# A four-layer attention network: queries, keys and values of two layers as seven products of halves

## The chip, the cores and the metric

The kernel runs on one core of one Trainium2 chip. The metric is the device time of one execution in microseconds (us); the time given is the median of several runs. The core has five instruction streams that work side by side and wait for each other by semaphores: PE (TensorE, the matrix products), DVE (VectorE), ACT (ScalarE), POOL (GpSimd) and SP (SyncE, here only for starting transfers).

## What is computed

The input x is 2 images of 512 channels and 32 x 32 = 1024 positions. Four layers follow one another; layers 0 and 1 are not touched by the change (layer 0: deformable attention with a learned bias and an MLP; layer 1: linear attention). Layers 2 and 3 are two attention blocks of one form:

```python
def layer(x, gn_w, gn_b, qkv_w, qkv_b, proj_w, proj_b):   # layer 2: 8 groups; layer 3: 32 groups
    xn = group_norm(x) * gn_w + gn_b                      # x: (2, 512, 1024)
    q, k, v = qkv_w @ xn + qkv_b                          # each (2, 512, 1024), 8 heads of 64
    attn = softmax(q.T @ k * 64 ** -0.5)                  # per head, 1024 x 1024
    out = v @ attn.T                                      # (2, 512, 1024)
    return x + proj_w @ out + proj_b
```

Everything is float32.

## The kernel before

An image is held in SBUF as 4 tiles of 128 channels x 1024 positions (`self.xs[b][t]`). P is 128, C 512, CT 4, N 1024, HF 512, DH 64, NB 8; b counts images, t or c tiles of channels, h halves of 512 positions.

Layers 2 and 3 each run `attention` (from line 945). It calls `queries_keys_values` (982), then branches on a flag, computed on the chip, that says whether the logits are small enough to leave out the maximum of the softmax: with these data it always takes `heads_bounded` (1123), and `heads_general` is not executed.

`queries_keys_values` for each image: the norm (`group_norm`, 1110) writes 4 tiles; each block of 128 x 512 takes one subtraction and scaling on DVE (line 1117) and then the addition of the bias on ACT (1120). For each t the queries and then the keys are made: per half of the positions one PSUM accumulation over the 4 channel tiles (line 1016, 4 products of 128x128 weights with 128x512 data), taken out by DVE with bias and the factor 1/8 for a query (1024), or by ACT with the bias for a key (1028). POOL squares each finished 128x1024 tile (1032) and DVE takes block maxima of it (1034); from these the flag is made at the fourth block of the values (1046 to 1061). The values follow, 8 blocks of 128 positions x 512 channels, again 4 products each (1064), taken out by DVE with the bias `vb` (1071). The statistics of image 1 (`channel_means`, `group_means`, lines 1087 to 1105) are computed in the middle of image 0's first products; two small matmuls with `avg` (1094, 1101) average over a group.

`heads_bounded` works in 16 units: image b, pair of heads p, half h. A unit has 8 steps n. In each, PE makes the scores of 128 keys against 512 queries for both heads (line 1146), ACT takes the exponential out of PSUM (1150), POOL and DVE add the exponentials up (1155 to 1164), and PE, two steps later, multiplies them with the values (1175). PSUM holds 2 score tiles. At the end ACT and DVE add the two halves of o into the memory of the queries (1184, 1185). In step 4 of the next unit `divide` follows: PE sums over keys (1192), ACT copies one half (1196), DVE adds the other, takes the reciprocal and multiplies (1197, 1198, 1200). After all 16 units come the 8 projections (598), each added to x by DVE (607); in layer 2 the statistics of layer 3 are computed beside them, in layer 3 each piece of x is sent to DRAM at once.

The order on an engine is the order of the program where `manual_schedule` names the engine (DVE in `queries_keys_values`, PE in `heads_bounded`); elsewhere a scheduler of the framework places instructions when the kernel is built. An engine runs its instructions in that order and waits at the first that is not ready.

Layer 0's MLP already has the scheme that the change extends: `left_sums` (623), `right_sums` (631) and `seven` (638), with this table of left and right operand:

```python
SEVEN = {"P1": (0, 0), "P2": (1, 2), "P3": (6, 3), "P4": (3, 6), "P5": (2, 4), "P6": (4, 5), "P7": (5, 1)}
```

The left matrix has quarters a11, a12, a21, a22 and three sums S2, S3, S4 (index 0 to 6; S1 takes the place of a21), the right one quarters r0 to r3 and three sums. Each product covers half of the contraction, 2 instead of 4 channel tiles.

The weights of layer 2 and 3 (`attention_weights`, 930) are loaded by SP: 4 tiles of 128 x 1536 for queries, keys and values and 4 of 128 x 512 for the projection; layer 2's while the MLP of layer 0 runs, layer 3's while layer 2 runs.

Of the kernel before, what the change touches and what calls it, by code (L numbers as in the profile page):

```python
# [36 lines left out]
    ("gn_w2", CT), ("gn_b2", CT), ("qb2", CT), ("kb2", CT), ("pb2", CT),  # L37
    ("gn_w3", CT), ("gn_b3", CT), ("qb3", CT), ("kb3", CT), ("pb3", CT),
# [14 lines left out]
class Net:  # L53
# [569 lines left out]
    def left_sums(self, eng, w):  # L623

        a11, a12, a21, a22, s2, s3, s4 = (w[:, i] for i in range(7))
        eng.tensor_tensor(s3, a11, a21, ALU.subtract)
        eng.tensor_tensor(a21, a21, a22, ALU.add)
        eng.tensor_tensor(s2, a21, a11, ALU.subtract)
        eng.tensor_tensor(s4, a12, s2, ALU.subtract)
# [22 lines left out]
    def mlp0(self):  # L652
# [5 lines left out]
        with ExitStack() as ctx:  # L658
# [7 lines left out]
            def weights(n):  # L666
                got = []
                for name in ("mlp_w1", "mlp_w2"):
                    w = wpool.tile([P, 7, 2, 2 * P], F32, tag=name, name=f"{name}_{n}")
                    nc.sync.dma_start(w[:, 0:4], io[name][n % CT])  # L670
                    self.left_sums(nc.gpsimd, w)
# [258 lines left out]
    def attention_weights(self, pool, k: int, name: str):  # L930

        got = []
        for t in range(CT):
            src = self.io[f"l{k}_{name}"][t]
            got.append(pool.tile(list(src.shape), F32, tag=name, name=f"{name}{k}{t}"))
            self.nc.sync.dma_start(got[-1], src)
        return got
# [7 lines left out]
    def attention(self, k: int, qkv, proj, out, meanwhile=lambda: None):  # L945
# [3 lines left out]
        with ExitStack() as ctx:  # L949
            one = self.pool(ctx, f"a{k}")  # L950
            vb = one.tile([P, C], F32, tag="vb", name=f"vb{k}")
            nc.sync.dma_start(vb, self.io[f"l{k}_vb"].partition_broadcast(P))
# [3 lines left out]
            for b in range(B):  # L956
                qs = [one.tile([P, N], F32, tag=f"q{b}{t}", name=f"q{k}{b}{t}") for t in range(CT)]
                ks = [one.tile([P, N], F32, tag=f"k{b}{t}", name=f"k{k}{b}{t}") for t in range(CT)]
                v = one.tile([P, NB, C], F32, tag=f"v{b}", name=f"v{k}{b}")
                data.append((qs, ks, v))  # L960
            small_logits, got = self.queries_keys_values(k, qkv, vb, ones, data, meanwhile)
# [3 lines left out]
            with self.tc.If(small_logits > 0) as cmp:  # L965
                self.heads_bounded(k, ones, data, proj, out)
            with cmp.Else():
                self.heads_general(k, data)
                with ExitStack() as ctx2:
                    ps = self.pool(ctx2, f"a{k}_ps_p", 2, psum=True)  # L970
# [11 lines left out]
    def queries_keys_values(self, k, qkv, vb, ones, data, meanwhile):  # L982
# [4 lines left out]
        nc = self.nc  # L987
        with ExitStack() as ctx:
            act = self.pool(ctx, f"a{k}_x", 2)
            small = self.pool(ctx, f"a{k}_s", 2)  # L990
            squares = self.pool(ctx, f"a{k}_sq")
            ps = self.pool(ctx, f"a{k}_ps", 6, psum=True)
            ps_g = self.pool(ctx, f"a{k}_psg", 1, psum=True)
            flag = small.tile([1, B], F32, tag="flag", name=f"flag{k}")
            with self.tc.manual_schedule(engines={mybir.EngineType.DVE}):
                xns = [self.group_norm(k, 0, act)]
                for b in range(B):
                    xn = xns[b]
                    qs, ks, v = data[b]
                    late = []  # L1000
                    cm = squares.tile([P, 2, CT, DH], F32, tag="cm", name=f"cm{k}{b}")
                    for t in range(CT):
                        if b == 0 and t == 1:
                            for c in range(CT):
                                self.channel_means(k, 1, c)
                            self.means_tiles(k, 1)
                            for _ in self.group_means(k, 1, ps_g.tile([P, 2, CT], F32, tag="g0", name=f"gm{k}")):
                                pass
                            xns.append(self.group_norm(k, 1, act))
                        for i, y in enumerate((qs[t], ks[t])):  # L1010
                            at = i * C + t * P
                            for h in range(2):
                                cut = slice(h * HF, (h + 1) * HF)
                                acc = ps.tile([P, HF], F32, tag="ps", name=f"qk{i}p{k}{b}{t}{h}")
# [423 lines left out]
```

## Time and profile before

| what | value |
|---|---|
| median of 3 runs | 3492.95 us (3492.63 to 3493.12) |
| the profiled execution | 3491.61 us |
| its span in the profile | 3489.8 us |
| granted TensorE clock, mean | 0.996 |
| layer 0's attention | 0 to about 2089 us |
| layer 0's MLP | to 2474 us |
| layer 1 | 2474 to 2547 us |
| layer 2: queries, keys, values | 2548.7 to 2720.6 us |
| layer 2: attention and projection | 2721.5 to 3017.7 us |
| layer 3: queries, keys, values | 3019.2 to 3191.4 us |
| layer 3: attention, projection, output | 3192.2 to 3489.8 us |

The profile is one execution on the chip, told from its start in microseconds. A row of a group of instructions has the line of the program, the engine, the operation, what it writes and reads, the shapes and the count, then busy us and the mean in ns, then the idle time of the engine ahead of it and what ended that idle time. A row of waits has the engine and the tile that waited, what it waited for, the total, the number of times and the longest. A row of the chain or of the order in time has start and length in us. A float32 product of the program shows as two matmul records and two weight loads (LDWEIGHTS, "PEld"), which overlap with matmuls. A record's busy time includes its way through the array, so a dense sequence is priced by the distance of starts and not by the mean of one.

### The profile page before, as it was taken

Reading aid. Unit: us, or ns where it says so; the run is one execution under the profiler, and the core shown is the slowest. Engines: PE = TensorE matmul, PEld = TensorE weight load, DVE = VectorE, ACT = ScalarE, POOL = GpSimd, SP = SyncE. Lnnn points to the kernel's source line nnn. Section 1 sums busy time; section 2 is a strip of 40 time slices with the busy share of each in tenths; the row PEclk is TensorE's granted clock in tenths of the full one; section 3 lists DMA queues with packets and bytes.
Section 4 is the critical chain, followed back from the end, with each engine's and each line's share of the span. In section 5 each row is a group of like instructions: output and inputs, shape, how many; then the busy total and the mean of one; then the engine's idle time right before and its main releaser. Section 6 shows DMA issues by size and latency. Waiting matters only on the chain.

```text
span 3489.8 us, 59510 instructions
## 1 busy us (share of the span) xinstructions
PE 3433.0 (98%) x25152; PEld 1234.1 (35%) x25152; DVE 2235.6 (64%) x2393; ACT 2012.0 (58%) x2093; POOL 2016.5 (58%) x1512
## 2 busy tenths in 40 slices
PE   7999999999999999999999999999999999999999
PEld 2333333333333333333333334444644333443333
DVE  6877767767767578768766755565542566423774
ACT  5877877887887587887887741111120565102661
POOL 4777777787786577787788873332121344012441
PEclk9999999999999999999999999999999999999999
DMA  6877777787786677787888751110000000000001
GB/s 153 157 144 155 153 153 145 155 162 146 152 162 131 121 154 146 153 163 144 177 161 160 152 147 65 48 38 23 1 3 0 37 1 1 16 0 1 1 1 50
DMA packets 104108, 343.14 MB, mean 98 GB/s; under 512 B 12816, under 2 KB 14480, under 8 KB 101520
## 3 DMA queue, kind: packets, MB, share of 16 engines
q0 software_dynamic: 73296, 266.90, 40.4%
q1 hardware_dynamic: 29520, 70.21, 6.7%
q8 instruction: 202, 3.31, 0.4%
q10 hardware_dynamic: 1008, 2.06, 0.2%
q14 instruction: 82, 0.67, 0.1%
HBM read 67.79 MB, written 4.46 MB: 21 GB/s over the span
## 4 chain that ended last, share of the span: by engine, by line
PE 90%; DVE 7%; ACT 1%; issue 1%; POOL 0%; DMA 0%; DVEq 0%; ACTq 0%; POOLq 0%
PE hp L486 45%; PE o L1175 6%; PE s L1146 6%; DVE h L455 3%; PE qk0p L1016 3%; PE pb L598 3%; PE vp L1064 3%; PE qk1p L1016 3%; PE sim L518 3%; PE m_0P L647 1%; PE m_7P L647 1%; PE m_6P L647 1%; PE m_4P L647 1%; PE m_3P L647 1%; PE m_1P L647 1%; PE m_5P L647 1%
## 5 line engine op out<-in xcount | busy, mean ns | idle before, releaser
L486 PE MATMUL hp<-h,w 128*32 128x512 f32 x16384 | 1830.9, 593 | 5.6 <-DVE h L455 3.6
L455 DVE CUSTOM_DVE_ANT_1 h<-tx,bank 128x1024 f32<-128x1024 f32 x1024 | 1181.0, 1216 | 332.1 <-PE hp L486 309.0
L491 ACT ACTIVATE h<-hp,magb 128x1024 f32<-128x1024 f32 x1024 | 1122.0, 1111 | 416.5 <-PE hp L486 415.4
L486 PEld LDWEIGHTS hp<-h,w 128*32 128x32 f32 x16384 | 542.4, 110 | 1216.8 <-issue 1121.8
L478 POOL DMA_DIRECT2D h<-h x509 | 452.7, 1027 | 390.6 <-ACT h L497 333.2
L504 POOL TENSOR_TENSOR h<-h,h 128x1024 f32<-128x1024 f32 x255 | 613.9, 2408 | 21.3
L502 POOL TENSOR_SCALAR h<-h,flip 128x1024 f32<-128x1024 f32 x256 | 449.3, 1755 | 0.9 <-ACT h L491 0.9
L1150 ACT ACTIVATE e<-s 128x1024 f32<-128x1024 f32 x256 | 258.6, 1023 | 152.9 <-PE s L1146 152.8
L493 ACT ACTIVATE h<-h,flip 128x1024 f32<-128x1024 f32 x256 | 291.3, 1138 | 0.0
L1146 PE MATMUL s<-q,k 64*64 64x512 f32 x2048 | 259.9, 590 | 5.1 <-ACT e L1150 3.3
L1175 PE MATMUL o<-e,v 64*64 64x512 f32 x2048 | 260.8, 592 | 0.0
L1157 POOL TENSOR_TENSOR some<-some,e 128x1024 f32<-128x1024 f32 x64 | 151.3, 2365 | 82.6 <-ACT e L1150 80.2
L1155 POOL TENSOR_TENSOR some<-e,e 128x1024 f32<-128x1024 f32 x32 | 75.9, 2371 | 211.0 <-ACT q L1184 139.1
L495 POOL TENSOR_SCALAR h<-h,flip 128x1024 f32<-128x1024 f32 x128 | 145.6, 1137 | 76.4 <-ACT h L491 75.3
L1032 POOL TENSOR_TENSOR sq<-q 128x1024 f32<-128x1024 f32 x16 | 30.3, 1894 | 234.1 <-DVE q L1024 154.5
L1028 ACT ACTIVATE k<-qk1p,cols 128x512 f32<-128x512 f32 x32 | 22.0, 687 | 237.4 <-PE qk1p L1016 237.4
L497 ACT ACTIVATE h<-h,flip 128x1024 f32<-128x1024 f32 x128 | 145.6, 1137 | 0.0
L518 PE MATMUL sim<-h,ends 128*32 128x512 f32 x1024 | 141.0, 592 | 0.0
L1146 PEld LDWEIGHTS s<-q,k 64*64 64x64 f32 x2048 | 77.7, 133 | 148.0 <-issue 119.4
L1160 DVE TENSOR_TENSOR sum<-e,e 128x1024 f32<-128x1024 f32 x32 | 39.8, 1244 | 138.9 <-ACT e L1150 138.9
L1175 PEld LDWEIGHTS o<-e,v 64*64 64x64 f32 x2048 | 75.3, 133 | 146.7 <-issue 124.1
L1016 PE MATMUL qk0p<-xn,qkv 128*128 128x512 f32 x256 | 119.0, 617 | 8.3 <-ACT xn L1120 8.3
(367 smaller groups left out, 3074.9 us busy)
## 6 DMA issues: line engine op xcount, KB each, us to landing
h<-h POOLq DMA_DIRECT2D x509, 512.0 KB, 6.5
lb<-logs SPq DMA_DIRECT2D x63, 512.0 KB, 5.3
mlp_w<-in_mlp_w SPq DMA_DIRECT2D x16, 1024.0 KB, 4.8
qkv<-in_l_qkv SPq DMA_DIRECT2D x8, 768.0 KB, 6.0
x<-in_x SPq DMA_DIRECT2D x8, 512.0 KB, 9.3
out<-x SPq DMA_DIRECT2D x16, 256.0 KB, 2.1
proj<-in_l_proj SPq DMA_DIRECT2D x8, 256.0 KB, 6.4
l1w<-in_l_w SPq DMA_DIRECT2D x1, 1280.0 KB, 10.0
```

What stands on the lines that cost most here:

```text
L455: self.nc.vector._custom_dve(TENSOR_ADD_SAT, out=h[:, k, :, :], in0=x[:, jj, 2 * r + k, :].unsqueeze(1).to_broadcast([P, H, W]), in1=y[:, ...
L478: nc.gpsimd.dma_start(to, what, accum_op=ALU.add)
L486: nc.tensor.matmul(hp[rows, cut], lhsT=self.l0w2[:, 32 * q : 32 * q + 32], rhs=h1[k][:, cut], start=True, stop=True)
L491: nc.scalar.activation(y, hp, AF.Relu, bias=self.magb[:, q : q + 1])
L493: nc.scalar.activation(ys[0], ys[0], AF.Copy, scale=self.flip[:, 0:1])
L502: nc.gpsimd.tensor_scalar(y, y, self.flip[:, 2:3], 1.0, ALU.mult, ALU.mult)
L504: (nc.vector if final else nc.gpsimd).tensor_tensor(y, y, ys[2], ALU.add)
L518: nc.tensor.matmul(sims[u][at : at + 32, :], lhsT=self.ends[:, 28 - 4 * o : 60 - 4 * o], rhs=z[jj][:, h * HF : (h + 1) * HF], start=(o == ...
L1016: nc.tensor.matmul(acc, lhsT=qkv[c][:, at : at + P], rhs=xn[c][:, cut], start=(c == 0), stop=(c == CT - 1),)
L1146: nc.tensor.matmul(s[halves[c], par, :], lhsT=ks[p][rows, at : at + DH], rhs=qs[p][rows, cut], start=True, stop=True)
L1150: nc.scalar.activation(e, s, AF.Exp)
L1175: nc.tensor.matmul(o[halves[par], r, :], lhsT=v[rows, n, at : at + DH], rhs=e[rows, par, :], start=(n == 0), stop=(n == NB - 1),)
```

## The change

Both layers get the scheme of seven products. The 512 channels of the contraction and the positions are cut in halves, the output channels too (for queries and keys: the first half of the outputs is the queries, the second the keys; for values, the positions are the left side's place and the channels the right one's). In detail:

- `queries_keys_values` makes queries and keys together, 7 products x 4 tiles of outputs x 2 channel tiles, of 128x512 each, and then the values, 7 x 2 x 2 x 2 products of 128x256. The sums that the scheme needs of the weights are made on POOL (4 per weight matrix), those of the normed data on DVE (4 of 128x1024 per image).
- Seven results are put together into four blocks: most of them by a DVE addition from PSUM, P1 and P3 by ACT, one of P6 by POOL (`gather`).
- The norm of a block is one operation, x times a scale plus an offset that is computed once (`offsets_of_norm`); image 0's blocks are shared between DVE and ACT, image 1's are made on ACT during image 0's values.
- Squares and their maxima are taken per half tile (128x512).
- The factor 1/8 moves from the query into the exponential. The bias of the values moves out of the values: it is added to the divided result of a unit, by ACT.
- The statistics of image 1 come in parts behind P3, P6 and P7; the flag is computed behind the last values.
- In `queries_keys_values` the order of PE, ACT, DVE and POOL is now that of the program. The weights of the projection are loaded behind the branch.

```diff
-            with self.tc.manual_schedule(engines={mybir.EngineType.DVE}):
-                xns = [self.group_norm(k, 0, act)]
+            left_side(0)
+            def norm(b, r, i, c, eng):
+                t = 2 * (i // 2) + c
+                _, sc, off = self.means[b]
+                x = self.xs[b][t][:, (i % 2) * HF : (i % 2 + 1) * HF]
+                if eng is act:
+                    act.activation(r[i][:, c, :], x, AF.Identity, scale=sc[:, t : t + 1], bias=off[:, t : t + 1])
+                else:
+                    vec.tensor_scalar(r[i][:, c, :], x, sc[:, t : t + 1], off[:, t : t + 1], ALU.mult, ALU.add)
+            def queries_keys(b, r, which, t):
+                a, ri = SEVEN[which]
+                acc = ps.tile([P, HF], F32, tag="ps", name=f"qk{k}{b}{which}{t}")
+                for c in range(2):
+                    nc.tensor.matmul(
+                        acc, lhsT=left[0][a][:, c, t * P : (t + 1) * P], rhs=r[ri][:, c, :], start=c == 0, stop=c == 1
+                    )
+                y = blocks(b, t)
+                if which == "P1":
+                    act.activation(y[2], acc, AF.Identity, bias=self.col(f"kb{k}", t))
+                elif which == "P2":
+                    vec.scalar_tensor_tensor(y[0], acc, dqk[:, t : t + 1], y[2], ALU.add, ALU.add)
+                elif which == "P3":
+                    act.activation(y[1], acc, AF.Identity, bias=dqk[:, t : t + 1])
+                else:
+                    gather(which, acc, y)
+            def values(b, r, which, p):
+                a, ri = SEVEN[which]
+                acc = ps.tile([P, 2, 2 * P], F32, tag="ps", name=f"vp{k}{b}{which}{p}")
+                for n in range(2):
+                    at = (2 * p + n) * P
+                    for c in range(2):
+                        nc.tensor.matmul(
+                            acc[:, n, :], lhsT=r[ri][:, c, at : at + P], rhs=left[1][a][:, c, :], start=c == 0, stop=c == 1
+                        )
...
+            def gather(which, acc, y):
+                if which == "P5":
+                    vec.tensor_tensor(y[3], acc, y[2], ALU.add)
+                    vec.tensor_tensor(y[1], acc, y[1], ALU.add)
+                else:
+                    vec.tensor_tensor(y[2], acc, y[2], ALU.add)
+                    if which == "P6":
+                        nc.gpsimd.tensor_tensor(y[1], y[1], y[2], ALU.add)
...
+            engines = {getattr(mybir.EngineType, e) for e in ("PE", "Activation", "DVE", "Pool")}
+            with self.tc.manual_schedule(engines=engines):
+                self.offsets_of_norm(k, 0)
+                xns = [tiles(0)]
+                for i in (0, 2, 3, 1):
+                    for c in range(2):
+                        norm(0, xns[0], i, c, (vec, act)[c])
                 for b in range(B):
+                    r = xns[b]
+                    for which in ("P1", "P2", "P3", "P6", "P7", "P5", "P4"):
+                        if b == 0 and which == "P3":
+                            left_side(1)
+                        for t in range(CT):
+                            queries_keys(b, r, which, t)
+                            while len(late) > 1:
+                                late.pop(0)()
+                            for i, h in {"P2": [(0, 0)], "P5": [(0, 1), (1, 1)], "P4": [(1, 0)]}.get(which, []):
+                                while len(late) > 1:
+                                    late.pop(0)()
+                                late.append(square(i, t, h, cm))
+                            if b == 0 and which == "P3":
+                                self.channel_means(k, 1, t)
+                            if which == "P1" and t == 1:
+                                self.right_sums(vec, r)
+                        if b == 0 and which == "P3":
+                            self.means_tiles(k, 1)
+                            means = self.group_means(k, 1, ps_g.tile([P, 2, CT], F32, tag="g0", name=f"gm{k}"))
+                        elif b == 0 and which in ("P6", "P7"):
+                            next(means, None)
...
+                    for n, which in enumerate(("P1", "P2", "P3", "P6", "P7", "P5", "P4")):
+                        for p in range(2):
+                            values(b, r, which, p)
...
+                ok = small.tile([1, B], F32, tag="ok", name=f"ok{k}")
+                vec.tensor_scalar(ok, flag, 480.0**2, None, ALU.is_le)
+                oki = small.tile([1, 1], mybir.dt.int32, tag="oki", name=f"oki{k}")
+                vec.tensor_tensor(oki, ok[:, 0:1], ok[:, 1:2], ALU.mult)
+                early = small.tile([P, 1], F32, tag="early", name=f"early{k}")
+                act.activation(early, self.cols[:, 0:1], AF.Exp, scale=0.0)
...
+    def offsets_of_norm(self, k, b):
+        gm, sc, off = self.means[b]
+        self.nc.vector.tensor_tensor(off, gm, sc, ALU.mult)
+        self.nc.vector.tensor_tensor(off, self.colr(f"gn_b{k}", CT), off, ALU.subtract)
...
+            proj = self.projection_weights(self.pool(ctx, f"b{k}_w"), k)
...
-                nc.scalar.activation(e, s, AF.Exp)
+                nc.scalar.activation(e, s, AF.Exp, scale=DH**-0.5)
...
                 nc.vector.reciprocal(t, t)
                 res = data[b][0][p][:, h * HF : (h + 1) * HF]
                 nc.vector.tensor_tensor(res, res, t, ALU.mult)
+                nc.scalar.activation(res, res, AF.Identity, bias=self.col(f"vb{k}", p))
```

## The prediction

> **What bounds the kernel now.** I read the engine shares of the page first, then the waits of PE, then the busy time by stage, then the chain of waits through layers 2 and 3, and last the order in time inside one attention unit.
>
> ```profile
> PE 3433.0 (98%) x25152; PEld 1234.1 (35%) x25152; DVE 2235.6 (64%) x2393; ACT 2012.0 (58%) x2093; POOL 2016.5 (58%) x1512
> ```
>
> PE is busy 98% of the span, so only PE work removed, or PE idle time made, moves the end. The stage in question, layer 2 from its first product (2548.67) to its last (2720.60), cut into the four parts Q/K and V of image 0, Q/K and V of image 1:
>
> ```profile
> 2548.67:2608.44 59.77, 58.60 (x133) 25.81 (x134) 26.78 (x48) 14.27 (x23) 13.26 (x7) 0.96 0.02 4
> 2608.44:2637.05 28.61, 28.61 (x69) 12.16 (x69) 7.55 (x12) 0.69 (x1) 1.89 (x1) 1.00 0.00 0
> 2637.05:2691.99 54.94, 54.94 (x130) 24.33 (x129) 14.94 (x16) 4.81 (x7) 13.25 (x7) 1.00 0.00 0
> 2691.99:2720.60 28.61, 28.61 (x68) 11.81 (x67) 7.85 (x14) 0.89 (x2) 1.89 (x1) 1.00 0.05 13
> ```
>
> Columns: stretch, its length, then busy us of PE, weight loads, DVE, ACT, POOL, then granted clock. PE is full in three parts; DVE, ACT and POOL are at most 45% busy. Image 0's Q/K part is 4.8 us longer than image 1's. Layer 3 repeats this (60.03, 28.62, 54.93, 28.63). The waits of PE name part of it, and the chain gives the price of one matmul record (one product of the code is two records):
>
> ```profile
> PE qk0p L1016 <- ACT xn L1120: 8.3, 2, 5.0
> PE gm L1094 <- DVE mv L1088: 2.3, 2, 1.2
> PE s L1146 <- ACT e L1150: 3.3, 2, 1.7
> ```
>
> ```profile
> 2474.71 14.54 PE l1qk L812 x128
> 2499.00 7.15 PE m L857 x64
> ...
> 2643.92 6.87 PE qk1p L1016 x16
> ```
>
> 512 columns: 6.87/16 = 0.429 us a record. 128 columns: 14.54/128 = 0.114. 65 columns: 7.15/64 = 0.112.
>
> **The products.** Before, one image takes 128 records for Q/K and 64 for V. After: Q/K 7 x 4 x 2 = 56 products = 112 records of 512 columns, 112 x 0.429 = 48.1 us against 54.9. V: 7 x 2 x 2 x 2 = 56 products of 256 columns = 112 records. No row has 256 columns: half of 0.429 is 0.2147; the straight line between 128 and 512 columns gives 0.2188. I take 0.2165, so 24.25 us against 64 x 0.429 = 27.5. An image saves 6.87 + 3.2 = 10.1 us, four save 40.4 (39.4 to 41.2).
>
> A rule speaks against this. The Trainium skill, "TensorE: Matmul & The Clock Gate", Part 3, The mechanism, says that a weight load overlaps running matmuls only where the row groups differ, and its LDWEIGHTS section prices 128 columns at 107 ns. All these products use all rows, and V now needs twice as many loads per column streamed. By the rule 448 records would each show 0.107 us more: +48 us, and the change loses. But the 128-column row, which also reloads 128x128 weights every record, stands at 0.114, its streaming time (0.429/4 = 0.107) and 7 ns; 65 columns are no cheaper, so a load has a floor near 0.11, hidden under anything longer. I go by the rows.
>
> **Stalls of image 0.** It loses 4.8 us (layer 3: 5.1). About 2.6 are six records at 0.85 us each after the idle start (granted clock 0.96); they stay, since PE still waits for the norm. The rest is image 1's statistics, which stood in front of PE (the gm row). They move behind P3 and their matmuls behind P6 and P7, 6.9 us and more after DVE is free; about 0.45 us of small matmuls stays. Gain 1.8 a layer, 3.6 in all.
>
> **Start of a layer.** Two 128x4 operations (0.2 each) are added on DVE, but ACT no longer waits for DVE's half of the norm. I take 0.1 gain a layer.
>
> **What the seven products cost elsewhere.** DVE gets four 1.23 us sums of right halves an image and 36 evacuation steps of about 0.69 in place of 16; it goes from 57 to about 87 us in a stage of 149. POOL gets left sums (4 x 1.9 and 4 x 1.27) and twelve 1.27 us additions a layer, and 32 squares of about 1.27 for 16 of 1.9: from 30 to about 68. The tightest place is P5: DVE has 8 x 0.69 + 7 x 0.62 = 10 us, POOL 8 x 1.27 = 10 us, while PE makes the four products in 6.9. DVE falls some 4 us behind; six PSUM buffers of 1.72 us cover that, and P4 and P1 (ACT) let it catch up. Without that cover it would be 3 to 4 us an image. Left sums: layer 2's are queued on POOL right behind the MLP (2473.4), four of 1.9 and the memsets end near 2482.6, and the square of layer 1 is due at 2482.9; layer 3's run under the projection. Price zero; up to 1 us each if late. On SP, the loads of proj move behind the branch, 235 us ahead of their use; layer 1's weights move from among layer 0's last loads to behind the first four MLP loads, still 300 us early; layer 3's weights stay ahead of SP's own branch, which nobody waits for: zero each. The removed vb load and layer 0's one moved table load hid nothing from PE: zero.
>
> **The bias of V moves into attention, and this costs.** Each (image, pair, half) unit now ends with an Identity on ACT, in place, on what DVE has just divided. In the built order of the changed kernel ACT's sequence is, in 30 of the 32 units, copy r, exp, exp, Identity, exp. The rows of before for that place:
>
> ```profile
> 2789.28 0.58 ACT L1196 COPY r<-d 128x512 f32<-128x512 f32 x1 [0.72 <-PE d L1192]
> 2790.17 1.02 ACT L1150 ACTIVATE e<-s 128x1024 f32<-128x1024 f32 x1 [0.30 <-PE s L1146]
> 2791.92 1.03 ACT L1150 ACTIVATE e<-s 128x1024 f32<-128x1024 f32 x1 [0.73 <-PE s L1146]
> 2793.61 1.02 ACT L1150 ACTIVATE e<-s 128x1024 f32<-128x1024 f32 x1 [0.66 <-PE s L1146]
> ...
> 2790.63 3.35 DVE L1198 RECIPROCAL r<-r 128x512 f32<-128x512 f32 x1
> 2794.02 0.69 DVE L1200 TENSOR_TENSOR q<-q,r 128x512 f32<-128x512 f32 x1
> ...
> 2792.45 1.04 PE L1146 MATMUL s<-q,k 64*64 64x512 f32 x8
> 2795.88 1.04 PE L1146 MATMUL s<-q,k 64*64 64x512 f32 x8
> ```
>
> The Identity must wait for DVE's multiply, which ends at 2794.71 behind a 3.35 us reciprocal, while ACT is free at 2792.95. Behind it on ACT is the third exp, due at 2793.61. The Identity runs 2794.76 to 2795.4 (next group: 0.71 alone, about 0.62 to the next start), that exp ends near 2796.4 and not at 2794.63. Two score buffers exist, so the scores at 2795.88 need that exp's buffer: they start at about 2796.5.
>
> ```profile
> L1120 ACT ACTIVATE xn<-xn,cols 128x512 f32<-128x512 f32 x32 | 20.0, 708 | 9.4 <-DVE xn L1117 9.4
> ```
>
> PE stalls 0.6 us a unit; ACT recovers within two steps (1.02 of work in 1.72), so it neither grows nor vanishes. 30 x 0.6 = 18 us back. Low end 0 (if the built order did not bind), high end 0.9 (no overlap of the Identity, 0.2 of wake-up): 27. The last unit of each layer ends under 28 us of projections: zero.
>
> **The branch.** The flag was ready at 2705.30, 15 us ahead of the last product; ACT passed load and branch in 0.73. Now it stands behind DVE's last evacuation.
>
> ```profile
> 2705.15 0.15 DVE L1061 TENSOR_TENSOR oki<-ok 1x1 int32<-1x1 f32 x1
> 2706.03 0.20 ACT L1083 ACTIVATE early<-cols 128x1 f32<-128x1 f32 x1 [13.31 <-DVE oki L1061]
> 2722.67 1.28 ACT L1150 ACT_TABLE_LOAD   x1 [16.44 <-PE s L1146]
> ```
>
> From the last matmul's end: 0.73 evacuation, 0.37 for ok and oki, 0.73 load and branch, so first scores at +1.83 where they were at +0.88. In layer 2 a Sqrt table load (1.28 + 0.2) is queued ahead of the Exp load: the third score block starts at +5.7 where it was +4.4, 1.3 lost. In layer 3 the built order has the Exp table loaded ahead of the branch and none behind it: +4.1 against +4.5, 0.4 gained. Together 0.9 lost (0 to 4). The clock-gate section of the same page has the clock halve after about 3.4 us of idling; PE idles here 1.8 and 2.2 us, so by the rule nothing, and the rows of before (0.9 and 1.6 idle, clock 1.00) cannot show more. Were it to halve, 2.6 us a layer.
>
> **Sum.** 40.4 + 3.6 + 0.2 - 18 - 0.9 = 25.3 us. The profiled execution took 3491.6 (span 3489.8 and 1.8 around it), so 3466.3; the median of the runs is 1.3 above it: 3467.6.
>
> **Rivals.** (1) The Identity is hidden: ACT is only 62% busy in attention. Against it: the order is in-line and the dates above leave it no gap. It gives 3449.6. Chance 0.13. (2) The Identity hurts more: DVE's add into q ends at 2799.27 and PE's next o at 2799.32 waits for its buffer, no slack; a later sum chain could add 0.3 to 0.5 us a unit, 9 to 15 us: 3477 to 3483. For it: two just-in-time hand-overs; against: the chain shifts with the scores, about 0.15 left. Chance 0.12. (3) DVE or POOL become the bound of the seven products (P5 not covered): 3 to 4 us an image, about 14: 3481. Against: a stage 60% busy and six buffers. Chance 0.05. (4) Slower than before: V's weight loads show, as the rule has it. The place is the 448 records of 256 columns; the price 0.107 each, 3515; it decides from 25.3/448 = 0.056 us exposed a record. Chance 0.04. The case of the sum keeps 0.66.
>
> **Numbers.** A measurement of this kernel tells about 0.2% (7 us) from no change. The sum's own bounds (Identity 0.45 to 0.9, branch 0 to 4, records 39.4 to 41.2) span 3463 to 3480; with rival 1 the range is 3449 to 3480, which leaves out rival 4 and the tails of 2 and 3. Slower only rival 4 (0.04); within 0.2% a mixture of 2 and 3 (0.03); faster 0.93.
>
> **What would show it.** Right: Q/K parts of about 48.1 us and V parts of about 25.2, each with PE full and clock 1.00; no wait on mv; V records with starts 0.217 apart; in attention a new wait of PE scores on ACT exp of about 0.6 us in 30 places, units of 15.3 us where they were 14.7. Wrong: Identity without a PE wait behind it; V records beyond 0.27; PE waiting on DVE or POOL inside P5 to P4.

## The result and the profile after

The changed kernel takes 3471.72 us (median of 4 runs, 3469.07 to 3472.31), the kernel before 3493.03 beside it: a ratio of 0.9938, 95% interval 0.9921 to 0.9955, 21.3 us less. The forecast was 3467.6. The profiled execution took 3472.31 us with a span of 3470.5, and it is the slowest of the four.

The parts of layer 2 first: Q/K and V of image 0, Q/K and V of image 1, in the profile after. The columns are those of the same view before.

```profile
2553.39:2604.91 51.52, 51.52 (x117) 22.96 (x118) 35.51 (x62) 8.08 (x14) 23.78 (x22) 0.94 0.00 1
2604.91:2630.25 25.34, 25.34 (x118) 21.33 (x117) 13.27 (x23) 8.21 (x12) 5.34 (x5) 1.00 0.00 0
2630.25:2678.32 48.07, 48.07 (x114) 21.31 (x113) 27.52 (x40) 5.50 (x8) 18.68 (x18) 1.00 0.00 1
2678.32:2703.76 25.44, 25.42 (x117) 21.08 (x115) 12.30 (x21) 3.83 (x6) 5.31 (x5) 1.00 0.22 83
```

PE has no gap left in any of the four, DVE is busy for 48 to 69% of them, and image 1's Q/K and both V have the length of their count of records: 48.07 us for 112 records of Q/K, 25.3 to 25.5 for V. Image 0's Q/K is longer and has a mean clock of 0.94. Layer 3 gives 50.35, 25.47, 48.00 and 25.36.

The waits of PE after, from which those of layers 0 and 1 are left out:

```profile
PE s L1229 <- ACT e L1233: 11.2, 30, 0.8
...
PE qk30P L1046 <- issue: 4.2, 1, 4.2
PE s L1229 <- DVE oki L1141: 3.7, 2, 2.0
...
PE qk20P L1046 <- DVE xn L1028: 2.9, 1, 2.9
...
PE o L1258 <- ACT e L1233: 2.4, 2, 1.2
```

Of the 30 times in the first row 28 are new. The other two stand right behind the branch, where the row of before has two as well (`PE s L1146 <- ACT e L1150: 3.3, 2, 1.7`). The last row, one wait of 1.2 us a layer, is new too. The order in time inside one attention unit shows where it comes from (ACT, then DVE, then PE):

```profile
2760.72 0.58 ACT L1279 COPY r<-d 128x512 f32<-128x512 f32 x1 [0.69 <-PE d L1275]
2761.61 1.02 ACT L1233 ACTIVATE e<-s 128x1024 f32<-128x1024 f32 x1 [0.30 <-PE s L1229]
2763.36 1.02 ACT L1233 ACTIVATE e<-s 128x1024 f32<-128x1024 f32 x1 [0.73 <-PE s L1229]
2766.18 0.72 ACT L1284 ACTIVATE q<-q,cols 128x512 f32<-128x512 f32 x1 [1.80 <-DVE q L1283]
2766.81 1.92 ACT L1233 ACTIVATE e<-s 128x1024 f32<-128x1024 f32 x2
...
2776.00 0.58 ACT L1279 COPY r<-d 128x512 f32<-128x512 f32 x1 [0.72 <-PE d L1275]
...
2762.07 3.35 DVE L1281 RECIPROCAL r<-r 128x512 f32<-128x512 f32 x1
2765.45 0.69 DVE L1283 TENSOR_TENSOR q<-q,r 128x512 f32<-128x512 f32 x1
...
2766.48 1.04 PE L1258 MATMUL o<-e,v 64*64 64x512 f32 x8
2767.87 1.09 PE L1229 MATMUL s<-q,k 64*64 64x512 f32 x8 [0.34 <-ACT e L1233]
```

ACT stands 1.80 us at the Identity, the exponential behind it runs late, and the scores that need its buffer start 1.39 us after the group before them, where a dense sequence has 0.86. The bracket says only 0.34, since a record's busy time includes its way through the array: a stall of PE is read from the distance of starts. A unit, from one copy of the denominators to the next, is 2776.00 - 2760.72 = 15.28 us. Before it was 14.68:

```profile
2759.90 0.58 ACT L1196 COPY r<-d 128x512 f32<-128x512 f32 x1 [0.67 <-PE d L1192]
...
2774.58 0.58 ACT L1196 COPY r<-d 128x512 f32<-128x512 f32 x1 [0.69 <-PE d L1192]
```

Over all units of both layers the median is 15.25 us after and 14.67 before, so a unit costs 0.58 us more.

Cut at the same first records in every kernel's profile (layer 0's attention; its MLP; layer 1 to its w products; from there to the first product of layer 2; from there to the first scores; to the first product of layer 3; to its first scores; to the end), the span divides as follows, to about 0.1 us. The table has the experiments too.

| kernel | layer 0 | MLP | layer 1 | w | L2 q, k, v | L2 attention | L3 q, k, v | L3 attention |
|---|---|---|---|---|---|---|---|---|
| before | 2089.0 | 385.7 | 50.7 | 23.3 | 172.8 | 297.7 | 173.0 | 297.6 |
| after | 2091.4 | 385.7 | 51.9 | 24.4 | 152.3 | 307.4 | 150.9 | 306.5 |
| e1 bias on DVE | 2091.1 | 385.7 | 51.9 | 24.3 | 152.4 | 302.8 | 150.9 | 301.1 |
| e2 before + Identity | 2091.0 | 385.7 | 50.7 | 23.3 | 172.8 | 307.7 | 173.2 | 307.1 |
| e3 Identity later | 2094.0 | 385.7 | 51.8 | 22.5 | 151.0 | 295.9 | 150.8 | 296.9 |
| e4 left sums late | 2091.4 | 385.7 | 50.7 | 27.6 | 151.2 | 310.3 | 150.7 | 306.5 |
| e5 flag early | 2093.7 | 385.8 | 51.8 | 22.6 | 149.7 | 306.6 | 150.0 | 306.5 |
| e6 V by eight | 2093.8 | 385.7 | 50.7 | 24.6 | 158.7 | 307.0 | 157.5 | 305.7 |
| e7 e3 + e4 + e5 | 2090.2 | 385.7 | 50.7 | 27.7 | 150.0 | 299.8 | 150.4 | 296.4 |
| e8 no bias | 2090.4 | 385.8 | 51.8 | 25.0 | 151.7 | 297.3 | 152.3 | 296.9 |
| e9 three edits | 2089.3 | 385.7 | 50.7 | 23.3 | 150.7 | 295.9 | 151.0 | 296.8 |
| e10 sums in the MLP | 2091.0 | 385.7 | 50.7 | 23.8 | 151.2 | 306.6 | 150.8 | 306.3 |

Layers 2 and 3 give 20.5 and 22.1 us at their products and take 9.7 and 8.9 back in their attention. Layer 1, which the change does not touch, is 1.2 us longer. Two columns move without a cause in the code, and both go with the granted clock. Layer 0's attention ends at 2089.0 to 2091.0 in the three profiles in which the clock stays full from 150 us to that end (before, e9, e10), at 2090.2 to 2091.4 in the six with one stretch of 3.4 us at half clock near 205 us, and at 2093.8 to 2094.0 in the three with a second one near 2080 us (e3, e5, e6). This row of the profile after holds its one stretch (mean clock 0.91); before has 1.00 there:

```profile
200.00:220.00 20.00, 17.19 (x168) 5.82 (x164) 16.29 (x19) 12.70 (x14) 12.53 (x11) 0.91 0.69 132
```

The w stage has a long stretch of half clock in every profile, and its length goes with it: 13.7 us where the stage takes 22.5 (e3, e5), 17.1 where it takes 23.3 to 23.8 (before, e2, e9, e10), 20.5 where it takes 24.3 to 25.0 (after, e1, e6, e8; e4 and e7 also have 20.5, and another cause that is told below). The mean clock is the last column but two in these rows of before, after and e3:

```profile
2536.00:2562.00 26.00, 22.73 (x41) 9.84 (x40) 10.98 (x23) 9.04 (x17) 10.65 (x8) 0.67 0.05 11
...
2536.00:2562.00 26.00, 22.10 (x35) 9.32 (x35) 15.57 (x31) 9.38 (x16) 10.10 (x8) 0.61 0.00 1
...
2536.00:2562.00 26.00, 22.10 (x41) 9.23 (x41) 18.04 (x35) 9.78 (x16) 9.99 (x8) 0.74 0.00 1
```

### The profile page after: what moved, and what is told of

Same layout as the page of the kernel before. It is cut to its first block, busy times and chain, and to the rows that moved or that the text cites. A ratio compares the mean times of both kernels' runs of the same rounds, so it can differ in the third digit from the quotient of the medians.

```text
span 3470.5 us, 60111 instructions
## 1 busy us (share of the span) xinstructions
PE 3403.5 (98%) x25280; PEld 1260.8 (36%) x25280; DVE 2296.9 (66%) x2507; ACT 2034.2 (59%) x2132; POOL 2078.3 (60%) x1584
## 4 chain that ended last, share of the span: by engine, by line
PE 88%; DVE 7%; ACT 2%; POOL 1%; issue 1%; DMA 0%; ACTq 0%; DVEq 0%; SPq 0%; POOLq 0%
PE hp L486 45%; PE s L1229 6%; PE o L1258 6%; DVE h L455 3%; PE pb L598 3%; PE sim L518 3%; PE qk20P L1046 1%; PE qk30P L1046 1%; PE m_0P L649 1%; PE m_5P L649 1%; PE m_3P L649 1%; PE m_2P L649 1%; PE qk31P L1046 1%; PE qk21P L1046 1%; PE m_6P L649 1%; PE m_1P L649 1%
## 5 line engine op out<-in xcount | busy, mean ns | idle before, releaser
L504 POOL TENSOR_TENSOR h<-h,h 128x1024 f32<-128x1024 f32 x255 | 613.6, 2406 | 21.3
L1240 POOL TENSOR_TENSOR some<-some,e 128x1024 f32<-128x1024 f32 x64 | 151.2, 2362 | 85.8 <-ACT e L1233 83.4
L1034 POOL TENSOR_TENSOR sq<-q 128x512 f32<-128x512 f32 x32 | 33.2, 1039 | 144.2 <-DVE q L1053 100.1
L708 ACT ACTIVATE mh<-mh,cols 128x512 f32<-128x512 f32 x64 | 46.2, 722 | 124.2 <-DVE mh L726 65.5
L628 POOL TENSOR_TENSOR mlp_w<-mlp_w 128x512 f32<-128x512 f32 x16 | 22.4, 1400 | 161.1 <-DMA mlp_w<-in_mlp_w 125.5
```

Of the source, the lines that this page charges most:

```text
L504: (nc.vector if final else nc.gpsimd).tensor_tensor(y, y, ys[2], ALU.add)
```

## The experiments

**The disputed term: the Identity in the order of ACT.** The theory is that it costs by its place, in front of an exponential and behind DVE's division. The rivals are that ACT has no time for it anywhere, and that the units are longer for another reason. Four kernels tell these apart.

e2 puts the Identity alone into the kernel before. Its operand is the queries' bias, since that kernel has no other column there, so its output is not the network's; the work on ACT is the same:

```diff
                 nc.vector.tensor_tensor(res, res, t, ALU.mult)
+                nc.scalar.activation(res, res, AF.Identity, bias=self.col(f"qb{k}", p))
```

> The kernel before with one line more: the Identity on ScalarE behind each unit's multiply, with the queries' bias as its operand, since there is no other column there (a wrong bias is added to each head's output; the work is the same as in the changed kernel). Theory (the Identity alone costs 0.59 us a unit, whatever else is changed): 3493.0 + 18 = 3511 us, units of 15.26. Rival (it costs only together with the other edits): 3493 to 3495.

Measured: 3512.41 us (3512.14 to 3513.34), ratio to before 1.0055 (1.0038 to 1.0072), 19.5 us more. The table has 10.0 and 9.5 in the two attentions and at most 0.2 in the other stages of layers 1 to 3; layer 0 is 2.0 longer in this profile, with the stretch of half clock near 205 us. PE's waits in this kernel:

```profile
PE s L1146 <- ACT e L1150: 13.2, 30, 1.7
...
PE o L1175 <- ACT e L1150: 2.4, 2, 1.2
```

So the Identity alone makes the whole give-back: 28 new waits of PE's scores, 14 a layer (the other two of the 30 are those behind the branch), and one of 1.2 us a layer in front of the values of the last unit, which the forecast had put at zero.

e3 leaves it on ACT, one exponential later. ACT joins the engines whose order is written out in `heads_bounded`:

```diff
-                nc.scalar.activation(res, res, AF.Identity, bias=self.col(f"vb{k}", p))
+                state["res"] = res
+
+            def shift(unit):
+                b, p, h, state = unit
+                nc.scalar.activation(state["res"], state["res"], AF.Identity, bias=self.col(f"vb{k}", p))
...
-            with self.tc.manual_schedule(engines={mybir.EngineType.PE}):
+            with self.tc.manual_schedule(engines={mybir.EngineType.PE, mybir.EngineType.Activation}):
...
                         divide(steps[i - NB][0])
+                    if i % NB == 7 and NB < i < len(steps):
+                        shift(steps[i - NB][0])
...
```

> The changed kernel with the same Identity on ScalarE, but one exponential later in its order (behind the fourth exponential after the copy of the denominators instead of the third); ScalarE's order in the attention is written out for that. Theory (the cost is the wait in the order, not ScalarE's time): the multiply ends before ScalarE comes to the Identity, nothing waits, units of 14.67 to 14.75, 3452 to 3456 us. Rival (ScalarE has no 0.72 us to spare between two exponentials, wherever it stands): units stay at 15.2 to 15.3, 3470 to 3473.

Measured: 3450.05 us (3449.78 to 3450.51), ratio 0.9877 (0.986 to 0.9893). ACT's order in time in a unit of this kernel:

```profile
2756.88 0.59 ACT L1279 COPY r<-d 128x512 f32<-128x512 f32 x1 [0.69 <-PE d L1275]
...
2761.26 1.03 ACT L1233 ACTIVATE e<-s 128x1024 f32<-128x1024 f32 x1 [0.72 <-PE s L1229]
2762.34 0.72 ACT L1288 ACTIVATE q<-q,cols 128x512 f32<-128x512 f32 x1
2762.97 1.00 ACT L1233 ACTIVATE e<-s 128x1024 f32<-128x1024 f32 x1
...
2771.59 0.59 ACT L1279 COPY r<-d 128x512 f32<-128x512 f32 x1 [0.72 <-PE d L1275]
```

The same 0.72 us Identity has no wait in front of it, the next exponential starts 0.63 behind it, and the unit is 14.71 us (the median of all is 14.68). ACT had the room; the cost was the order. The written order did one thing more: the load of the square root's table for layer 3's norm, which the builder had placed right ahead of layer 2's first exponential, now runs at the end of layer 2's attention. That is part of the 295.9 in the table, where e8, without an Identity but with that load, has 297.3.

e1 gives the addition to DVE:

```diff
-                nc.scalar.activation(res, res, AF.Identity, bias=self.col(f"vb{k}", p))
+                nc.vector.tensor_scalar(res, res, self.col(f"vb{k}", p), None, ALU.add)
```

> The changed kernel with one line other: the bias of the values is added by VectorE right behind its multiply, not by ScalarE. Theory (the addition costs because it stands in ScalarE's order in front of an exponential and waits there for VectorE's division): a unit of the attention takes 14.67 us again instead of 15.26, so 30 x 0.59 = 18 us come back, and the late exponentials at the end of each layer (1.2 each) may go too: 3471.7 - 18 to 20 = 3452 to 3454 us. Rival (the units are longer for another reason, such as the scale in the exponential or the values in four tiles): 3471 to 3472, units of 15.26. Second rival (VectorE is the tighter engine: 0.4 to 0.7 us more a unit on it delay the sums): units of 14.9 to 15.3, 3460 or more.

Measured: 3462.29 us (3460.79 to 3462.79), ratio 0.9911 (0.9895 to 0.9928). It lies between the first expectation (3452 to 3454) and the unchanged time, so the second rival holds for half of it. DVE in a unit of this kernel, and what PE waits for instead:

```profile
2764.72 0.69 DVE L1283 TENSOR_TENSOR q<-q,r 128x512 f32<-128x512 f32 x1
2765.44 0.49 DVE L1284 TENSOR_SCALAR q<-q,cols 128x512 f32<-128x512 f32 x1
2765.84 2.55 DVE L1245 TENSOR_TENSOR sum<-sum,e 128x1024 f32<-128x1024 f32 x2
2768.50 1.23 DVE L1247 TENSOR_TENSOR sum<-sum,some 128x1024 f32<-128x1024 f32 x1
2769.64 0.68 DVE L1268 TENSOR_TENSOR q<-o,q 128x512 f32<-128x512 f32 x1
```

```profile
PE o L1258 <- DVE q L1268: 6.4, 28, 0.2
```

From the reciprocal to the addition of o's halves DVE has no gap, and the next unit's o, of which there is one buffer, waits for that addition. A unit takes 15.05 us in the median. DVE is 71% busy over these units (140.40 us of the 196.40 from 2753.60 on) and yet has no 0.49 us to spare in this part of a unit. The forecast's second rival had named exactly this hand-over, with "no slack"; the changed kernel does not hit it, this one does.

e8 leaves the addition of the values' bias out, and so a part of what is computed.

> The changed kernel with no addition of the values' bias at all in the attention of layers 2 and 3 (that part of the computation is left out). It is the floor for any place of the addition. Theory (the later Identity costs nothing): the same as with the later Identity, 3450 us within 1, units of the same length. Rival (the later one still costs something): 3444 to 3448, and then that is what is left to gain; or, if the late order of ScalarE itself helped, more than 3450.

Measured: 3452.81 us (3452.01 to 3457.82), ratio 0.9886 (0.987 to 0.9903). Layer 3's attention is 296.9 us here and 296.9 in e3, and the median unit 14.68 in both: the later Identity costs nothing that can be seen, and the written order of ACT by itself gives a unit nothing. e8 is 2.8 us slower than e3 as a whole; its profile is longer by the table load (1.4), in the w stage (25.0 against 22.5) and in layer 3's products (152.3 against 150.8), and 3.6 shorter in layer 0. The last three go with the clock: layer 3's products start with 6.8 us at half clock here, with 3.4 in e3.

**The products.** e6 goes back to eight products for the values alone: `values` makes 8 blocks of 512 columns from normalized blocks that are kept in an eighth tile, and `left_side(1)` goes.

```diff
+            def values(b, r, n):
+                acc = ps.tile([P, 2, 2 * P], F32, tag="ps", name=f"vp{k}{b}{n}")
+                at = n % 4 * P
+                for c in range(CT):
+                    nc.tensor.matmul(
+                        acc,
+                        lhsT=r[c // 2 * 2 + n // 4][:, c % 2, at : at + P],
+                        rhs=weights[1][:, c // 2 :: 2, c % 2, :],
+                        start=(c == 0),
+                        stop=(c == CT - 1),
+                    )
...
```

> The changed kernel with the values by eight products of halves again (512 columns to a matmul, four to a block, from normalized blocks that are kept), queries and keys by seven as they are; the weights' sums for the values go, and the norm, the bias and the attention stay. Theory (a matmul of 256 columns hides its weight load: 0.2165 us a record): an image's values take 64 records x 0.429 = 27.5 us instead of 112 x 0.2165 = 24.25, so 4 x 3.2 = 12.8 us are lost: 3484 us. Rival (records of 256 columns with a load for each are dearer than that): 3472 or less.

Measured: 3480.70 us (3480.11 to 3485.49), ratio 0.9964 (0.995 to 0.9978), 9 us above the changed kernel; the stages say 6.4 + 6.6 = 13.0 for the products. Part of the difference is known: with one tile more in that pool the builder put layer 2's left sums into the MLP, and layer 1 is back at 50.7, 1.2 less; the two attentions are 1.2 shorter. 32 records in a row in this kernel and, second, in the changed one (start, length from the first start to the modelled end):

```profile
2606.03 13.90 PE L1064 MATMUL vp<-vw,xn 128*128 128x512 f32 x32
```

```profile
2604.87 7.07 PE L1065 MATMUL vp20P<-vw,xn 128*128 128x256 f32 x32
```

Half the columns take half the time, though each record has a weight load in both kernels. From one start to the next it is 0.216 us in the median where e6 has 0.429. The seven products of the values are worth 13.0 us as counted (12.8 forecast).

**Layer 1.** The builder puts layer 2's left sums on GpSimd ahead of layer 1's squares. GpSimd's order in time after:

```profile
2475.85 2.40 POOL L628 TENSOR_TENSOR qkm<-qkw 128x1024 f32<-128x1024 f32 x1
2478.32 2.35 POOL L629 TENSOR_TENSOR qkw<-qkw 128x1024 f32<-128x1024 f32 x1
2480.76 2.41 POOL L630 TENSOR_TENSOR qkm<-qkw 128x1024 f32<-128x1024 f32 x1
...
2484.28 2.40 POOL L631 TENSOR_TENSOR qkm<-qkw,qkm 128x1024 f32<-128x1024 f32 x1
2486.63 1.90 POOL L825 TENSOR_TENSOR sq<-qk 128x1024 f32<-128x1024 f32 x1
```

With the whole run 2.4 us later than before, the first square was due at 2485.30 and starts at 2486.63. e4 moves the pool of the sums one place up, so that their memory is free only after layer 1:

```diff
+            sums = self.pool(ctx, f"a{k}_w")
             small = self.pool(ctx, f"a{k}_s", 2)
             xpool = self.pool(ctx, f"a{k}_x")
             squares = self.pool(ctx, f"a{k}_sq", 2)
-            sums = self.pool(ctx, f"a{k}_w")
```

> The changed kernel with the pool of the weights' sums opened one place earlier, so that it lies in memory that layer 1 still uses: GpSimd then makes layer 2's four left sums behind layer 1's last additions and no longer in front of layer 1's memsets and squares; nothing else moves on any engine. Theory (the four sums of 2.4 us delay the squares by 1.3 us, and the whole of layer 1 with them): from layer 1's first products of queries and keys to its w products 50.7 us as in the kernel before instead of 51.9, a gain of 1.2 us in that stage, and layer 2's start no later (the sums end 9.6 us into it, the first is used by the third product, 13.7 us in): about 3470.5 us. Rival (layer 1's loss is the clock's, not the sums'): 51.9 us there as now. Second rival (the sums come too late for the third product, or hold up GpSimd's squares): a wait of some us in front of the third product.

Measured: 3476.20 us (3475.93 to 3477.35), ratio 0.9951 (0.9934 to 0.9967): 4.5 us slower than the changed kernel, a miss. Layer 1 does return to 50.7, but the w stage grows to 27.6 and layer 3 starts later too, since its sums moved to its start as well. GpSimd and DVE at the start of layer 2 in this kernel:

```profile
2552.59 2.34 POOL L629 TENSOR_TENSOR qkw<-qkw 128x1024 f32<-128x1024 f32 x1
2555.01 2.47 POOL L630 TENSOR_TENSOR qkm<-qkw 128x1024 f32<-128x1024 f32 x1
2557.57 2.46 POOL L631 TENSOR_TENSOR qkm<-qkw,qkm 128x1024 f32<-128x1024 f32 x1
...
2552.57 8.20 DVE L1028 TENSOR_SCALAR xn<-x,sc,off 128x512 f32<-128x512 f32 x4
```

```profile
PE qk20P L1046 <- DVE xn L1028: 7.1, 1, 7.1
```

The four operations of the norm, 1.92 us together after, take 8.20: three of them last 2.6 us each and end some 0.3 us behind the sum of GpSimd beside them. The operation on 128x4 just ahead of them (line 1203) takes 2.19 us instead of 0.16 in the same way. PE waits 7.1 us instead of 2.9. I had asked whether the sums would be late for PE and not whether they would shut DVE out. The Trainium skill, "SBUF — State Buffer", section "Who interferes with whom", has it: GpSimd and DVE, where DVE works in a mode with two ports, share a pair of ports, and whoever starts first keeps it for the whole instruction. This trace agrees that the two shut each other out, with 2.62 us for a norm operation that takes 0.54 alone; which of them started first, and that the norm works in that mode, no row tells.

e10 splits the pool instead, which lets the sums run in the MLP:

```diff
-            sums = self.pool(ctx, f"a{k}_w")
+            sums = [self.pool(ctx, f"a{k}_w{i}") for i in (1, 0)]
...
-                more = sums.tile([P, 3, 2, w.shape[3]], F32, tag=name, name=f"{name}m{k}")
+                more = sums[1 - i].tile([P, 3, 2, w.shape[3]], F32, tag=name, name=f"{name}m{k}")
```

> The changed kernel with the pool of the weights' sums split in two, so that the queries' and keys' sums lie in memory that is free early: GpSimd then makes layer 2's four left sums in the MLP, behind the sums of its second pair of weights, and not in front of layer 1's squares. Theory (the four sums cost layer 1 its 1.2 us, and at layer 2's start they cost more since VectorE's norm and GpSimd's sums shut each other out there): 50.7 us from layer 1's first products to its w products instead of 51.9, layer 2's first product 2.9 us after the means as now (7.1 with the sums at that place), the MLP no longer than before: 3470.5 us. Rival (in the MLP they delay the next weights or the x additions): the MLP's 385.7 us from its first product to layer 1's first grow by 1 us or more, and nothing is won.

Measured: 3468.47 us (3467.94 to 3468.91), ratio 0.993 (0.9913 to 0.9946). Its GpSimd rows:

```profile
2098.59 2.40 POOL L628 TENSOR_TENSOR qkm<-qkw 128x1024 f32<-128x1024 f32 x1 [8.05 <-DMA qkw<-in_l_qk]
...
2484.93 1.89 POOL L825 TENSOR_TENSOR sq<-qk 128x1024 f32<-128x1024 f32 x1 [7.79 <-DVE qk L817]
```

The sums wait only for their weights, the square only for its data, the MLP stays at 385.7 and layer 1 at 50.7. The 1.2 us are the sums' place, and free where GpSimd had idle time. Of the 3.3 us between the medians (4.4 between the profiles) that is 1.2. The rest lies where the profiles differ in the clock: 0.4 in layer 0, 0.6 in the w stage, 1.1 in layer 2's first products (3.5 us at half clock, 5.8 after) and 0.8 behind the branch, where this profile has the full clock.

**The branch.** e5 moves the two operations of the flag up:

```diff
                             self.largest(k, b, ones, cm, small, ps_g, flag)
+                            if b == B - 1:
+                                ok = small.tile([1, B], F32, tag="ok", name=f"ok{k}")
+                                vec.tensor_scalar(ok, flag, 480.0**2, None, ALU.is_le)
...
-                ok = small.tile([1, B], F32, tag="ok", name=f"ok{k}")
-                vec.tensor_scalar(ok, flag, 480.0**2, None, ALU.is_le)
...
```

> The changed kernel with the two operations that make the branch's flag right behind the maxima of the second image, no longer behind the last sum of the values. Theory (TensorE waits at the branch for the flag): from the last product to the first scores 0.9 us as in the kernel before instead of 1.7 to 2.0, a gain of 0.8 to 1.1 us in each of layers 2 and 3: about 3469.7 us. Rival (the wait is for the branch itself, or the exponentials set the pace there): first scores 1.7 to 2.0 us after as now, or earlier scores with the third block no earlier.

Measured: 3468.49 us (3468.36 to 3469.59), ratio 0.9928 (0.9912 to 0.9945). PE behind layer 2's last product, first after, then e5:

```profile
2705.72 3.49 PE L1229 MATMUL s<-q,k 64*64 64x512 f32 x16 [1.97 <-DVE oki L1141]
2710.03 2.00 PE L1229 MATMUL s<-q,k 64*64 64x512 f32 x16 [0.83 <-ACT e L1233]
```

```profile
2703.64 1.95 PE L1230 MATMUL s<-q,k 64*64 64x512 f32 x16 [0.88 <-DVE v L1084]
2707.29 2.00 PE L1230 MATMUL s<-q,k 64*64 64x512 f32 x16 [1.70 <-ACT e L1234]
```

The gap is 0.88 as before, so 1.1 us come back at the first scores, and 0.9 in layer 3; layer 2's third block, which waits for an exponential, comes 4.5 us after the last product (6.3 after). The changed kernel's first two blocks ran at half the clock in that profile (3.49 us, as e1's 3.40 and e6's 3.54; 1.95 in e3, e4, e8 and e10 with the same gap), so 0.7 of that difference is not the flag's. The run is 3.2 us below the changed kernel; the flag's part of that is 2.0.

**Together.** e7 joins e3, e4 and e5, and was forecast before e4's result was known.

> The three edits together: the Identity one exponential later, the left sums behind layer 1, the flag behind the maxima. Theory (they act in different stages and add up): 3450.0 - 1.2 - 2 = 3446.8 us (3445 to 3449). Rival (a half clock at the start of layer 2 or the exponentials at the branch eat the small ones): 3449 to 3451.

Measured: 3454.02 us (3452.73 to 3454.18), ratio 0.9886 (0.987 to 0.9903): 7 above the expectation, slower than e3 alone. The stages name the cause, the left sums at the start of layers 2 and 3: 27.7 in the w stage, 299.8 in the column that holds layer 3's start. e9 takes e10's split in place of e4's edit:

> The Identity one exponential later, the flag behind the maxima, and layer 2's left sums in the MLP by the split pool. Theory (three places in three stages, which add up): 3450.0 - 2.0 (the flag, 1.0 a layer) - 1.2 (layer 1's squares) = 3446.8 us (3445 to 3448.5). Rival (the clock's half-speed stretch at the end of layer 1 or the first exponentials eat the small gains): 3449 to 3451.

Measured: 3446.53 us (3445.28 to 3448.45), ratio 0.9868 (0.9852 to 0.9885), 46.9 us below the kernel before beside it and 25 below the changed one. All of PE's waits from layer 2 on in this kernel:

```profile
PE qk30P L1046 <- DVE xn L1028: 4.2, 1, 4.2
PE qk20P L1046 <- DVE xn L1028: 2.9, 1, 2.9
PE s L1230 <- DVE v L1084: 1.8, 2, 0.9
PE s L1230 <- ACT e L1234: 0.9, 2, 0.4
```

Nothing is left there but the starts of the two layers (7.1 us) and the two branches (2.7).

## Why the prediction held, and where it was off

The mechanisms were right, the products' gain and the give-back of the Identity above all, and the time came out 4.1 us above the forecast, inside its range. That the sum came so close is in part luck, since some of its terms were off in opposite ways. By its own steps:

- **The products, 40.4 us.** Right. Q/K took 48.07 and 48.00 us for image 1 (48.1 forecast), V 25.34 to 25.47 (25.2). The distance of V's starts is 0.216 us, where 0.2165 was chosen. The rule of the Trainium skill that was set against this ("TensorE: Matmul & The Clock Gate", Part 3, The mechanism) would have shown as some 0.32 us a record; no part has it, and e6 confirms it from the other side. Loads are busy for 21.33 of the 25.34 us of image 0's V, 117 of them at some 0.18 us each (the rule was priced with 0.107), while PE stays full: loads and products run beside each other. The same section also lets a load be drawn ahead into a background weight buffer, which the prediction left out; no row tells whether that is what happens. The measurement decides: between dense records of 256 columns on all rows the load is hidden.
- **Stalls of image 0, 3.6 us.** Image 0's Q/K part fell by 59.77 - 51.52 = 8.25 in layer 2 and 60.03 - 50.35 = 9.68 in layer 3. Less 6.87 of products each, that is 1.4 and 2.8: 4.2 together. The two differ by the clock: layer 2 had 5.1 us of this part at half clock before and 5.8 after, layer 3 5.7 and 3.4. At half the rate that is an estimated 0.3 lost and 1.1 won, which leaves 1.7 us of stalls in each layer, against 1.8 forecast.
- **Start of a layer, 0.2 us.** It was more: PE's idle time ahead of the first product fell from 3.3 to 2.9 us in layer 2 and from 5.0 to 4.2 in layer 3.
- **Price zero for DVE, GpSimd and SP.** No wait of PE on DVE or GpSimd in the four parts, six buffers were enough. DVE had 88.6 us of work in layer 2's stage (87 forecast), GpSimd 53.1 and not 68, since four left sums lie ahead of the stage and a square of half a tile takes 1.04 us and not 1.27. But the left sums failed, by a term of the sum: the forecast had four of 1.9 us, from the squares' row, and an end at 2482.6, just ahead of the square. They took 2.4 each: a square, which reads one tile twice, is shorter than a sum of two tiles, and the row for the sum stood in the same page (L504, two tiles of that size, 2.4). The square came 1.3 us late and layer 1 lost 1.2; the text had said up to 1 us if late. e4, e6 and e10 show it by its absence.
- **The Identity, 18 us.** Right in mechanism and place; the size agrees because two errors cancel. There are 28 stalls and not 30, and a unit is 0.58 us longer, which makes 16.2. The last unit of each layer was put at zero; its late exponential is also what the last values wait for, and it is 1.4 us longer (16.38 against 14.95). Together that is 19.1, and e2 measured 19.5 for the Identity alone.
- **The branch, 0.9 us lost.** First scores 1.97 and 1.73 behind the last product (1.83 forecast). Third block 6.3 in layer 2 (5.7 forecast, and 5.6 in e10, where the clock did not halve) and 4.1 in layer 3 (4.1). A halved clock had been put at nothing, by the rule of 3.4 us of idling in the clock-gate section of the same page of the Trainium skill ("TensorE: Matmul & The Clock Gate"), or else at 2.6 us a layer. In the profile after it did halve behind 1.97 us, for 3.4 us, and cost 0.7. The measurement decides: 1.97 us of idling can be enough.
- **The sum.** For the profiled execution it gave 3466.3, and the clock and layer 1 make most of the difference of 6.0: 2.4 up to the end of layer 0, 1.2 in layer 1, 1.1 in the w stage. Layer 2 was to gain 11.8 up to layer 3's first product (40.4/4 x 2, 1.8 and 0.1, less 1.3 and 9.0) and gained 10.8; layer 3 was to gain 13.5 and gained 13.2. The 2.4 and the 1.1 lie in stages whose time varies by as much between profiles of the same code, and with the clock: after has 3.4 us at half clock in layer 0 where before has none, and 20.5 in and behind the w stage against 17.1. At half the rate that is up to 1.7 us each, an estimate; what sets the length of these stretches is not shown.
- **The rivals.** The hidden Identity was priced at 3449.6, and e3, which hides it, takes 3450.05. That this is so exact is luck: e3 also has layer 1's late square, 5.0 us more in layer 0 than before, no late last unit and no table load behind the branch. The second, DVE's hand-over of o, is real but starts only when DVE gets 0.49 us more a unit (e1). The third and fourth did not occur.

## What to carry to other kernels

Fewer products on a full PE are worth their count of records, and this can be forecast to some per cent; what is given back comes from where the by-products of the change are queued. Before an operation is put on an engine that is 60% busy, look at what stands behind it in that engine's order and at when its input is ready: one place later made 21.7 us here, the busier DVE only 9.4. Spare work of GpSimd belongs where DVE has nothing short to do that PE waits for, and the memory in which a pool lies can decide when the builder lets it start.

## What the runs showed of the hardware beyond this

A GpSimd sum of two different 128x1024 tiles takes 2.4 us and a square of one 1.9. While GpSimd sums ran without a gap, DVE's norm of a 128x512 block took up to 2.65 us, alone 0.54. The granted clock falls to 0.50 at the end of layer 1 in all twelve profiles, from at once (e8) to some 2.7 us (e3) behind PE's short waits of 0.3 and 0.7, and for 13.7 (e3), 17.1 (before) or 20.5 us (after). At the branch, 1.97 to 2.01 us of idling was followed by 3.4 us of half clock in three profiles (after, e1, e6) and by full clock in four (e3, e4, e8, e10); what decides it stays open.
